# One sorted expert group with weights fetched per tile, in a two-layer decoder planned by hand

## The chip, the cores and the metric

The kernel runs on one core of one Trainium2 chip. The metric is the device time of one execution in microseconds (us); the figure for a kernel is the median over several executions. A run can also be profiled: the profile's span goes from the first to the last instruction, and the profiled execution has a device time of its own, slightly longer than its span.

The engines are TensorE (PE, matrix products; its weight loads are shown apart as PEld), VectorE (DVE), ScalarE (ACT), GpSimd (POOL) and SyncE (SP, which only issues transfers). Each engine runs its own list of instructions strictly in order and waits on semaphores for the others.

## The reference, cut to what matters

The computation is a pre-norm decoder of two layers on x[16, 128, 256], all in fp32:

```
x = x + L0_attn(ln(x));   x = x + L0_xattn(ln(x), ctx);   x = x + L0_ffn(ln(x))
x = x + L1_attn(ln(x));   x = x + L1_xattn(ln(x), ctx);   x = x + L1_ffn(ln(x))
```

The change touches only the last term, a mixture of 8 experts of which each token uses 2, beside one shared expert:

```
shared = swiglu(x, ws_gate, ws_up, ws_down)                   # inner width 256
scores = sigmoid(x @ gate_weight.T)                           # (tokens, 8)
w, idx = top_k(scores, 2);  w = 2.5 * w / (w.sum(-1) + 1e-20)
y[e]   = (silu(x @ w_gate[e].T) * (x @ w_up[e].T)) @ w_down[e].T   # inner width 128
out    = sum over the two chosen e of w * y[e]  +  shared
```

## The kernel before, in words

**Lanes.** The 16 sequences of 128 tokens are cut into 8 lanes of two sequences (256 tokens each). A lane passes through `layer_0` (causal attention, attention to the context, a block-sparse FFN) and `layer_1` (self attention, windowed attention to the context, then the experts). Every stage is a Python generator.

**The planner.** The order of the instructions on every engine is fixed when the kernel is built. The class `Turns` (lines 81 to 262) holds all running generators as threads. A thread asks for an engine and for tiles from numbered pools (`yield PE, dict(bank=1)`); `run` picks the thread that could start first by a table of costs (`charge`, `dve`, `act`, `pool`, `indexed`), and breaks ties in favour of threads that are in an attention score step (`holds`, or a request for the score banks `s`), then by rank. So costs, tile limits (`LIMITS`) and the tie rule decide the order on PE, DVE, ACT, POOL and SP; on the chip each engine then keeps that order whatever the true durations are. `IN_FLIGHT` lanes (five) run at a time, started in the order of `TURN`.

**Two forms of the experts.** Dense (`expert_ffn`): all eight experts are computed for all tokens of a lane. Per lane that is 8 experts times 4 fp32 products for gate and up, a product `wb` that spreads the routing weight over the inner width, and 16 products down; the shared expert's products run in the same loops. Sorted (`routing`, then `sorted_experts`): for a group of lanes, `routing` scatters each token's normalised row to its two experts' areas of a DRAM table (`to_experts`, four indexed transfers per lane, POOL) and computes the shared expert as a dense part (`shared`). When the group's last lane is routed, `plan` (DVE) works out which rows belong to which tile of 128 rows, and the group's tiles are started. The number of tiles is fixed at 2·(tokens)/128 + 7, to hold any distribution over the experts. With GROUPS ((0,1,2),(3,4,5)) there are two groups of 12 + 7 = 19 tiles, and lanes 6 and 7 are dense.

**One sorted tile** (`expert_tile`, before): POOL gathers 128 rows (1 KB each) into `xg`; PE transposes them (2), ACT copies to `xgT`; PE reads the tile's expert number from SBUF into a register (`value`, line 158, a TENSOR_LOAD) and uses it as the column offset into the resident weights `gu` (two products); ACT and DVE form silu(gate)·up; PE transposes (`hT2`), ACT copies; PE multiplies with the resident `down` at the same register offset; ACT copies to `yo` and issues its transfer to `by_experts`. The resident weights (three tiles of 1 MB) are loaded by `late_weights` when the last lane has left layer 0, and a group may not start before they have landed (`ready`).

**Combining** (`combining`): after a group's last tile, each lane gathers its tokens' two results from `by_experts` (four indexed transfers on POOL), DVE adds them into x with their weight, and SP writes x out.

`blank` clears `to_experts` in eight transfers per group, so that unused rows are finite.

Of the kernel before, what the change touches and what calls it, by code (L numbers as in the profile page):

```python
# [10 lines left out]
I32 = mybir.dt.int32  # L11
# [7 lines left out]
P = 128  # L19
DC = D // P  # L20
G = 2
# [9 lines left out]
BPC = P // 64  # L31
NE, TOPE = 8, 2

GROUPS = ((0,1,2),(3,4,5))


OUT = -(2.0**100)
# [44 lines left out]
class Turns:  # L82
# [3 lines left out]

    HOP = 70.0
    HOP_FROM_PE = 200.0  # L90
    SWITCH = 91.0

    def __init__(self, nc, limits):
        self.nc = nc
# [60 lines left out]
        self.moves = max(self.moves, self.now.at) + n_bytes / 300.0  # L155
        self.now.at = self.moves + 2000.0

    def value(self, src, most):

        self.charge(PE, 300.0)  # L160
        return self.nc.values_load(
            src, engines=(mybir.EngineType.PE,), min_val=0, max_val=most,
            skip_runtime_bounds_check_because="a count of the experts but one, times their width",
        )

    def indexed(self, out, out_index, src, src_index):

        at = lambda i: None if i is None else bass.IndirectOffsetOnAxis(ap=i, axis=0)
        self.charge(POOL, 1100.0 if out_index is not None else 1600.0)
        self.moved(4 * int(np.prod((src if src_index is None else out).shape)))  # L170
        self.nc.gpsimd.indirect_dma_start(out, at(out_index), src, at(src_index))  # L171

    def fetch(self, out, src):
# [58 lines left out]
    def run(self, more):  # L232

        while True:
            more()
            best = None
            for i, th in enumerate(self.threads):
                if th.ask is None:
                    continue
                engine, takes = th.ask  # L240
                at = self.reach(th, engine)
                ok = True
                for tag, n in takes.items():
                    left = sorted(self.tiles[tag])
                    if not n:
                        continue
                    if len(left) < n:
                        ok = False
                        break
                    at = max(at, left[n - 1])  # L250
                key = (at, not (th.holds or "s" in takes), th.rank, i)
                if ok and (best is None or key < best[0]):
                    best = key, th, at
            if best is None:
                assert not self.threads, "no thread can go on"
                return
            _, th, at = best
            engine, takes = th.ask
            for tag, n in takes.items():
                self.tiles[tag].sort()  # L260
                del self.tiles[tag][:n]
            th.at, th.last = max(th.at, at), engine
            self.resume(th, None)


class Thread:
    def __init__(self, gen, rank, at, parent):
        self.gen, self.rank, self.at, self.parent = gen, rank, at, parent
        self.holds = parent is not None and parent.holds
        self.last, self.ask, self.waits, self.children, self.result = None, None, 0, [], None  # L270


# [1 line left out]
def decoder(ctx: ExitStack, tc: tile.TileContext, a: dict, out: bass.AP):  # L274
# [83 lines left out]
    class Sorted:  # L358
# [3 lines left out]
        def __init__(self, k, lanes):  # L362
            self.lanes, self.left = lanes, len(lanes)
            self.cap = cap = len(lanes) * GT
            self.tiles = n = TOPE * cap // P + NE - 1
            self.to_experts = dram.tile([NE * cap + P, D], F32, name=f"to_experts{k}")
            self.by_experts = dram.tile([n * P, D], F32, name=f"by_experts{k}")

            self.first_row = keep.tile([P, NE], F32, name=f"first_row{k}")
            self.next_row = keep.tile([P, NE], F32, name=f"next_row{k}")  # L370
            self.offset = keep.tile([P, NE], F32, name=f"offset{k}")

            self.tile_rows = keep.tile([P, n], I32, name=f"tile_rows{k}")
            self.tile_expert = keep.tile([P, n], I32, name=f"tile_expert{k}")
# [7 lines left out]


    LIMITS = dict(
        bank=4, s=2, oT=1, xn=5, xT=4, qk=5, qs=3, kb=3, v=3, p=4, oS=2, on=4, xe=6, hm=7, tmp=3, rank=2, selT=2, p0=3,
        pT0=3, unseen=4, chosen=3, swap=1, words=1, top=3,
    )
    q = Turns(nc, LIMITS)

# [146 lines left out]
    def attention(qT, kb, v, j, unseen=None, to=None):  # L536
# [5 lines left out]

        js = slice(j * S, (j + 1) * S)
        yield PE, dict(s=2)
        q.now.holds = True
        ss = banks()
        for e in range(DC):
            for r in range(4):
# [9 lines left out]
        for t2, s in enumerate(ss):  # L558
# [5 lines left out]
        q.now.holds = False  # L564
        yield PE, dict(bank=1)
        t = bank([P, S], "topT")
        q.transpose(t, top, ident)
# [12 lines left out]
        )  # L580
        q.give("tmp")
        yield PE, dict(s=2)
        q.now.holds = True
        ss = banks()
        for e in range(DC):
            for h in range(HR):
# [10 lines left out]
        def exponentials(s):  # L597
            yield ACT, dict(p=1)
            p = new("p", [P, HC, S], "p")
            q.act("activation", p, s.rearrange("p r h e s -> p (r h e) s"), AF.Exp)  # L600
            q.give("s")
            q.now.holds = False
            return p

        pTs = yield [exponentials(s) for s in ss]
        q.now.holds = False
        yield PE, dict(oT=1, bank=1)

        oT = bank([P, H // 4, S], "oT")
# [14 lines left out]
        q.act("copy", oS, oT)  # L624
        q.give("oT")
        q.give("bank")
        q.now.holds = False
        yield PE, dict(bank=1)
        o = bank([P, H // 4, S], "o")
        for t4 in range(H // 4):  # L630
# [412 lines left out]
    def plan(g):  # L1043
# [35 lines left out]
        q.dve("tensor_scalar", f, f, consts[:, C_ROW : C_ROW + 1], None, ALU.add)  # L1079
        q.dve("tensor_copy", g.tile_rows, f)  # L1080
        q.dve("tensor_scalar", e, e, float(D), None, ALU.mult)
        q.dve("tensor_copy", g.tile_expert, e)
        q.give("tmp", 3)

    def expert_tile(g, i):

        yield POOL, dict(xe=2)
        xg = new("xe", [P, D], "xg")
        q.indexed(xg, None, g.to_experts, g.tile_rows[:, i : i + 1])
        yield PE, dict(bank=1)  # L1090
        t = bank([P, DC, S], "xgt")
        for d in range(DC):
            q.transpose(t[:, d, :], xg[:, d * P : (d + 1) * P], ident)
        q.give("xe")
        yield ACT
        xgT = new("xe", [P, DC, S], "xgT")
        q.act("copy", xgT, t)
        q.give("bank")
        yield PE, dict(bank=1, tmp=1)
        gu = bank([P, 2, P], "gu2")  # L1100
        at = q.value(g.tile_expert[0:1, i : i + 1], (NE - 1) * D)
        for d in range(DC):
            q.matmul(gu, xgT[:, d, :], w["gu"][d][:, bass.ds(at, D)], start=d == 0, stop=d == DC - 1)
        q.give("xe")
        yield ACT
        sg = new("tmp", [P, P], "sg2")
# [12 lines left out]
        hT = new("pT0", [P, P], "hT")  # L1119
        q.act("copy", hT, t)  # L1120
        q.give("bank")
        yield PE, dict(bank=1, xe=1)
        y = bank([P, D], "y2")
        q.matmul(y, hT, w["down"][:, bass.ds(at, D)], start=True, stop=True)
        q.give("pT0")
        yield ACT
        yo = new("xe", [P, D], "yo")
# [3 lines left out]
        q.give("xe")  # L1131

    def combining(g, l):

        yield DVE
        t = small.tile([P, G, TOPE, NE], F32, tag="picked", name="picked", bufs=2)
        each = g.offset.unsqueeze(1).unsqueeze(1).to_broadcast([P, G, TOPE, NE])
        q.dve("tensor_tensor", t, pick[l], each, ALU.mult)
        f = small.tile([P, G, TOPE], F32, tag="wk", name="from", bufs=2)
        q.dve("tensor_reduce", f, t, AX.X, ALU.add)  # L1140
        q.dve("tensor_tensor", f, f, place[l], ALU.add)
        by = results[l]
        q.dve("tensor_copy", by, f.rearrange("p j k -> p (j k)"))

        def one(j, k):
            yield POOL, dict(xe=1)
            y = new("xe", [P, D], "yg")
            q.indexed(y, None, g.by_experts, by[:, j * TOPE + k : j * TOPE + k + 1])
            yield DVE
            q.dve(  # L1150
                "scalar_tensor_tensor", x[l][:, j, :], y, weight[l][:, j, k : k + 1], x[l][:, j, :], ALU.mult, ALU.add
            )
            q.give("xe")

        yield [one(j, k) for j in range(G) for k in range(TOPE)]
        nc.sync.dma_start(out[l * G : (l + 1) * G].rearrange("b s d -> s b d"), x[l])

    def blank(g):
# [235 lines left out]
    def layer_1(l):  # L1394
# [4 lines left out]
        if g is not None:  # L1399
            yield from routing(l)  # L1400
            g.left -= 1
            if g.left == 0:
                q.start(sorted_experts(g), 2 * NL + min(g.lanes), max([q.now.at] + ready))

    IN_FLIGHT = 5

    TURN = [(0, l) for l in range(6)]
    for l in range(NL):
        TURN += [(1, l), (0, l + 6)] if l + 6 < NL else [(1, l)]

    def more():
        n = begun[0]
# [51 lines left out]
def _layout(i):  # L1464
# [10 lines left out]
    def both_ways(mask):  # L1475
# [54 lines left out]
```

## Time and profile before

| what | value |
|---|---|
| median of 8 runs | 839.28 us (837.53 to 841.04) |
| device time of the profiled execution | 839.29 us |
| span of the profiled execution | 837.5 us |
| PE busy, share of the span | 777.4 us, 93% |
| PE weight loads busy | 609.6 us, 73% |
| DVE / ACT / POOL busy | 478.2 us, 57% / 393.6 us, 47% / 434.7 us, 52% |
| mean granted PE clock | 0.975 |
| bytes moved by DMA | 65.98 MB, 79 GB/s on average |

How to read the page: a group of instructions is named by its source line, engine, operation and tiles (`gu<-gu,xgT` writes gu from gu and xgT; buffer numbers are left out). Most operations go through the planner's helpers, so many groups share one line: L132 is every matmul, L137 every transpose, L141 every DVE, L145 every ACT, L151 every POOL compute operation, L171 every indexed transfer, L161 the register load. An fp32 matmul is recorded as two passes, so counts of fp32 products are twice those of the code; transposes are one pass each. A record's mean duration includes the pipeline's latency: the pitch at which passes follow each other is read from the chain of waits or the timeline instead. "Idle before" is the time the engine stood still just before the group and what released it.

### The profile page before, as it was taken

The page shows a single profiled execution, that of the slowest core. Times are in us where ns is not written, and L with a number is a line of the kernel's source. Part 1 is how long each engine was busy: PE and PEld are TensorE (multiplying, and loading weights), DVE is VectorE, ACT ScalarE, POOL GpSimd, SP SyncE. Part 2 cuts the span into 40 slices and gives each one's busy share as a digit, 9 for nine tenths or more (in the row PEclk, how much of TensorE's full clock was granted, in tenths as well). Part 3 has the DMA queues.
Part 4 walks back from the last instruction along what each step waited for, and adds up shares of the span by engine and source line. Part 5 has one row for each costly group of instructions (what it writes and reads, how often), then busy time and mean ns, then how long its engine had stood idle before and what let it go on. Part 6 is the DMA issues. An engine that isn't in the chain of part 4 may idle for free.

```text
span 837.5 us, 19964 instructions
## 1 busy us (share of the span) xinstructions
PE 777.4 (93%) x7864; PEld 609.6 (73%) x7864; DVE 478.2 (57%) x1261; ACT 393.6 (47%) x899; POOL 434.7 (52%) x693
## 2 busy tenths in 40 slices
PE   6999999999999999999798998999999788999992
PEld 5777678788778777787576777777777575687782
DVE  4445746545437337655476546697677367374343
ACT  4545563443265546525643545455545643542430
POOL 5334665235135448556549429586687455472304
PEclk9999999999999999999899998999999997999997
DMA  8446522412700010120002131111132122242214
GB/s 288 143 129 173 155 68 84 150 51 73 238 4 1 14 52 3 40 81 9 1 14 77 52 114 52 52 45 58 40 92 68 45 83 76 64 132 70 89 47 124
DMA packets 63582, 65.98 MB, mean 79 GB/s; under 512 B 9024, under 2 KB 56256, under 8 KB 62848
## 3 DMA queue, kind: packets, MB, share of 16 engines
q1 hardware_dynamic: 53888, 48.43, 18.5%
q0 software_dynamic: 4128, 11.28, 4.4%
q10 hardware_dynamic: 5472, 4.98, 1.8%
q8 instruction: 63, 1.03, 0.5%
q14 instruction: 31, 0.25, 0.1%
HBM read 35.31 MB, written 25.17 MB: 72 GB/s over the span
## 4 chain that ended last, share of the span: by engine, by line
PE 70%; DVE 11%; POOL 8%; ACT 5%; issue 4%; DMA 2%; ACTq 0%; POOLq 0%; DVEq 0%
PE s L132 14%; PE y L132 9%; PE pj L132 9%; PE pr L132 8%; PE gu L132 8%; PE hp L132 7%; PE oT L132 4%; PE tps L137 2%; DVE top L141 2%; POOL rstd L151 2%; PE o L137 2%; PE rt L132 2%; ACT p L145 1%; DMA yg<-by_experts,results 1%; POOL qs L151 1%
## 5 line engine op out<-in xcount | busy, mean ns | idle before, releaser
L141 DVE TENSOR_REDUCE top<-s 128x8 f32<-128x1024 f32 x96 | 112.9, 1217 | 54.8 <-PE s L132 54.5
L145 ACT ACTIVATE p<-s 128x1024 f32<-128x1024 f32 x96 | 93.1, 1022 | 58.8 <-PE s L132 58.8
L151 POOL TENSOR_TENSOR qs<-qT,less 128x512 f32<-128x512 f32 x48 | 61.1, 1278 | 89.5 <-ACT less L145 89.3
L151 POOL TENSOR_SCALAR rstd<-mv 128x2 f32<-128x2 f32 x72 | 17.9, 248 | 103.3 <-DVE mv L141 92.7
L132 PE MATMUL hp<-srcT,L_w 128*128 128x256 f32 x256 | 67.2, 392 | 0.1
L132 PE MATMUL s<-kb,qT 32*128 32x256 f32 x768 | 60.0, 412 | 1.3 <-DVE top L141 0.7
L132 PEld LDWEIGHTS s<-qs,kb 32*128 32x128 f32 x1536 | 48.5, 186 | 16.4 <-issue 8.1
L132 PE MATMUL s<-qs,kb 32*128 32x128 f32 x1536 | 58.1, 283 | 2.4 <-POOL qs L151 1.4
L171 POOL DMA_INDIRECT xg<-to_experts,tile_rows x38 | 37.6, 991 | 40.8 <-PE xgt L137 17.9
L132 PE MATMUL y<-L_w,hm 128*128 128x256 f32 x256 | 58.8, 382 | 0.0
L141 DVE SCALAR_TENSOR_TENSOR sg<-sg,gu 128x128 f32<-128x128 f32 (+1 forms) x70 | 24.0, 343 | 57.5 <-ACT sg L145 57.4
L132 PE MATMUL oT<-p,v 128*32 128x128 f32 x1536 | 52.9, 279 | 2.8 <-ACT less L145 1.0
L151 POOL TENSOR_SCALAR kb<-kT,consts 128x256 f32<-128x256 f32 x96 | 53.1, 565 | 3.4 <-ACT kT L145 2.5
L151 POOL TENSOR_TENSOR rstd<-rstd,power 128x2 f32<-128x2 f32 x72 | 51.4, 714 | 6.0
L132 PEld LDWEIGHTS hp<-srcT,L_w 128*128 128x128 f32 x256 | 45.5, 194 | 11.4 <-issue 2.2
L132 PEld LDWEIGHTS y<-L_w,hm 128*128 128x128 f32 x256 | 47.7, 190 | 7.5 <-issue 1.5
L145 ACT ACTIVATE hm<-hp,cols 128x256 f32<-128x256 f32 x64 | 26.8, 470 | 54.6 <-PE hp L132 54.2
L145 ACT ACTIVATE sg<-gu 128x128 f32<-128x128 f32 (+1 forms) x70 | 22.8, 326 | 59.4 <-PE gu L132 54.6
L132 PEld LDWEIGHTS oT<-p,v 128*32 128x32 f32 x1536 | 39.5, 111 | 14.5 <-issue 5.7
L132 PEld LDWEIGHTS s<-kb,qT 32*128 32x128 f32 x768 | 37.5, 189 | 16.5 <-issue 7.8
L145 ACT COPY oS<-oT 128x512 f32<-128x512 f32 x48 | 28.2, 588 | 43.1 <-PE oT L132 43.1
L137 PE MATMUL tps<-consts,xn 128*128 128x128 f32 x224 | 36.2, 284 | 11.4 <-DVE xn L141 7.0
(209 smaller groups left out, 1801.1 us busy)
## 6 DMA issues: line engine op xcount, KB each, us to landing
to_experts<-zero SPq DMA_DIRECT2D x14, 768.0 KB, 4.2
unseen<-hidden SPq DMA_DIRECT2D x128, 64.0 KB, 2.1
by_experts<-yo ACTq DMA_DIRECT2D x38, 128.0 KB, 1.7
c<-in_ctx SPq DMA_DIRECT2D x16, 256.0 KB, 3.6
x<-in_x SPq DMA_DIRECT2D x8, 256.0 KB, 6.3
L_w<-in_L_w SPq DMA_DIRECT2D x2, 1024.0 KB, 6.8
hidden<-plain SPq DMA_DIRECT2D x32, 64.0 KB, 1.6
swap<-kT SPq DMA_DIRECT2D x16, 128.0 KB, 2.1
```

Of the source, the lines that this page charges most:

```text
L132: self.nc.tensor.matmul(out, lhsT, rhs, **kw)
L137: self.nc.tensor.transpose(out, src, ident)
L141: getattr(self.nc.vector, name)(out, *args, **kw)
L145: getattr(self.nc.scalar, name)(out, *args, **kw)
L151: getattr(self.nc.gpsimd, name)(out, *args, **kw)
L171: self.nc.gpsimd.indirect_dma_start(out, at(out_index), src, at(src_index))
```

## The change

1. **Groups.** One sorted group of lanes 0 to 4 (2·1280/128 = 20, plus 7: 27 tiles) instead of two of three lanes (38 tiles); lanes 5, 6 and 7 are dense.
2. **Weights by indexed transfer.** A new input `L1_experts` holds each expert's gate, up and down weights as 128 rows of 3 KB. `plan` computes row numbers (`tile_weights` = 128·expert + partition) instead of a column offset (`tile_expert`). Each sorted tile gathers 128 x 3 KB of weights on POOL into a `p` buffer of 4 KB per partition, then gathers its tokens into the last 1 KB of the same buffer; the result `yo` overwrites the tokens, and the buffer is given back after the result's transfer. The register load on PE (`value`) is gone. The resident weights stay for the dense lanes.
3. **Combining** uses one `p` buffer per lane instead of four `xe` tiles.
4. **Planner.** Threads no longer carry `holds`; a request for `s` counts as 200 ns earlier (`LEAD`); PE is charged 40 ns more per turn (`PART`); an indexed transfer costs 1050 ns on POOL, and 2 us more until it is counted as landed. LIMITS: qs 3 to 2, p 4 to 6, xe 6 to 3, hm 7 to 5, tmp 3 to 4.
5. **Start order.** TURN starts seven lanes of layer 0 before the first of layer 1 (six before); the sorted group no longer waits for the resident weights.

```diff
-GROUPS = ((0,1,2),(3,4,5))
+GROUPS = ((0, 1, 2, 3, 4),)
...
+    LEAD = 200.0
+    PART = 40.0
...
-    def value(self, src, most):
-        self.charge(PE, 300.0)
-        return self.nc.values_load(...)
...
     def indexed(self, out, out_index, src, src_index):
-        self.charge(POOL, 1100.0 if out_index is not None else 1600.0)
+        self.charge(POOL, 1050.0)
         self.moved(4 * int(np.prod((src if src_index is None else out).shape)))
+        self.now.at += 2000.0
...
-                key = (at, not (th.holds or "s" in takes), th.rank, i)
+                first = "s" in takes
+                key = (max(at - self.LEAD * first, self.free_at[engine] - first), not first, th.rank, i)
...
+            if engine == PE:
+                self.free_at[PE] += self.PART
...
-        bank=4, s=2, oT=1, xn=5, xT=4, qk=5, qs=3, kb=3, v=3, p=4, oS=2, on=4, xe=6, hm=7, tmp=3, rank=2, selT=2, p0=3,
-        pT0=3, unseen=4, chosen=3, swap=1, words=1, top=3,
+        bank=4, s=2, oT=1, xn=5, xT=4, qk=5, qs=2, kb=3, v=3, p=6, oS=2, on=4, xe=3, hm=5, tmp=4,
+        rank=2, selT=2, p0=3, pT0=3, unseen=4, chosen=3, swap=1, words=1, top=3,
...
     def expert_tile(g, i):
-        yield POOL, dict(xe=2)
-        xg = new("xe", [P, D], "xg")
+        yield POOL, dict(p=1)
+        we = new("p", [P, HC, S], "we").rearrange("p h s -> p (h s)")
+        xg = yo = we[:, 3 * D :]
+        q.indexed(we[:, 0 : 3 * D], None, a["L1_experts"], g.tile_weights[:, i : i + 1])
+        yield POOL
         q.indexed(xg, None, g.to_experts, g.tile_rows[:, i : i + 1])
...
-        at = q.value(g.tile_expert[0:1, i : i + 1], (NE - 1) * D)
         for d in range(DC):
-            q.matmul(gu, xgT[:, d, :], w["gu"][d][:, bass.ds(at, D)], start=d == 0, stop=d == DC - 1)
+            wt = we[:, d * D : (d + 1) * D].rearrange("p (n f) -> p n f", f=P)
+            q.matmul(gu, xgT[:, d, :], wt, start=d == 0, stop=d == DC - 1)
...
-        q.matmul(y, hT, w["down"][:, bass.ds(at, D)], start=True, stop=True)
+        q.matmul(y, hT, we[:, DC * D : 3 * D], start=True, stop=True)
...
     def combining(g, l):
+        yield POOL, dict(p=1)
+        y = new("p", [P, G * TOPE, D], "yg")
         def one(j, k):
-            yield POOL, dict(xe=1)
-            y = new("xe", [P, D], "yg")
-            q.indexed(y, None, g.by_experts, by[:, j * TOPE + k : j * TOPE + k + 1])
+            yield POOL
+            q.indexed(y[:, i, :], None, g.by_experts, by[:, i : i + 1])
...
-                q.start(sorted_experts(g), 2 * NL + min(g.lanes), max([q.now.at] + ready))
+                q.start(sorted_experts(g), 2 * NL + min(g.lanes), q.now.at)
...
-    TURN = [(0, l) for l in range(6)]
+    TURN = [(0, l) for l in range(7)]
     for l in range(NL):
-        TURN += [(1, l), (0, l + 6)] if l + 6 < NL else [(1, l)]
+        TURN += [(1, l), (0, l + 7)] if l + 7 < NL else [(1, l)]
...
+    by_expert = lambda w: w.transpose(2, 0, 1, 3).reshape(NE, P, DC * D)
+        "L1_experts": np.concatenate([by_expert(gate_up), down.transpose(0, 2, 1)], 2).reshape(NE * P, 3 * D),
```

More of the change, by code (lines that the diff above doesn't have):

```diff
@@ L156, in moved @@
         self.now.at = self.moves + 2000.0
-    def value(self, src, most):
-        self.charge(PE, 300.0)
[L161 to L164, printed above, removed]
     def indexed(self, out, out_index, src, src_index):
         at = lambda i: None if i is None else bass.IndirectOffsetOnAxis(ap=i, axis=0)
-        self.charge(POOL, 1100.0 if out_index is not None else 1600.0)
+        self.charge(POOL, 1050.0)
         self.moved(4 * int(np.prod((src if src_index is None else out).shape)))
+        self.now.at += 2000.0
         self.nc.gpsimd.indirect_dma_start(out, at(out_index), src, at(src_index))
@@ L268, in __init__ @@
         self.gen, self.rank, self.at, self.parent = gen, rank, at, parent
-        self.holds = parent is not None and parent.holds
         self.last, self.ask, self.waits, self.children, self.result = None, None, 0, [], None
@@ L373, in __init__ @@
             self.tile_rows = keep.tile([P, n], I32, name=f"tile_rows{k}")
-            self.tile_expert = keep.tile([P, n], I32, name=f"tile_expert{k}")
+            self.tile_weights = keep.tile([P, n], I32, name=f"tile_weights{k}")
     groups = [Sorted(k, lanes) for k, lanes in enumerate(GROUPS)]
@@ L544, in attention @@
         yield PE, dict(s=2)
-        q.now.holds = True
         ss = banks()
@@ L563, in attention @@
             q.give("s")
-        q.now.holds = False
         yield PE, dict(bank=1)
@@ L582, in attention @@
         yield PE, dict(s=2)
-        q.now.holds = True
         ss = banks()
@@ L601, in exponentials @@
             q.give("s")
-            q.now.holds = False
             return p
         pTs = yield [exponentials(s) for s in ss]
-        q.now.holds = False
         yield PE, dict(oT=1, bank=1)
@@ L626, in attention @@
         q.give("bank")
-        q.now.holds = False
         yield PE, dict(bank=1)
@@ L1078, in plan @@
         q.dve("scalar_tensor_tensor", f, e, float(g.cap), f, ALU.mult, ALU.add)
[L1079 to L1082, printed above, removed]
+        for to, v in ((g.tile_rows, f), (g.tile_weights, e)):
+            if v is e:
+                q.dve("tensor_scalar", v, v, float(P), None, ALU.mult)
+            q.dve("tensor_scalar", v, v, consts[:, C_ROW : C_ROW + 1], None, ALU.add)
+            q.dve("tensor_copy", to, v)
         q.give("tmp", 3)
     def expert_tile(g, i):
-        yield POOL, dict(xe=2)
-        xg = new("xe", [P, D], "xg")
+        yield POOL, dict(p=1)
[3 more added lines that the diff above has]
+        yield POOL
         q.indexed(xg, None, g.to_experts, g.tile_rows[:, i : i + 1])
@@ L1093, in expert_tile @@
             q.transpose(t[:, d, :], xg[:, d * P : (d + 1) * P], ident)
-        q.give("xe")
-        yield ACT
+        yield ACT, dict(xe=1)
         xgT = new("xe", [P, DC, S], "xgT")
@@ L1121, in expert_tile @@
         q.give("bank")
-        yield PE, dict(bank=1, xe=1)
+        yield PE, dict(bank=1)
         y = bank([P, D], "y2")
-        q.matmul(y, hT, w["down"][:, bass.ds(at, D)], start=True, stop=True)
+        q.matmul(y, hT, we[:, DC * D : 3 * D], start=True, stop=True)
         q.give("pT0")
         yield ACT
-        yo = new("xe", [P, D], "yo")
         q.act("copy", yo, y)
@@ L1130, in expert_tile @@
         q.load(g.by_experts[i * P : (i + 1) * P, :], yo, engine=ACT)
-        q.give("xe")
+        q.give("p")
     def combining(g, l):
@@ L1143, in combining @@
         q.dve("tensor_copy", by, f.rearrange("p j k -> p (j k)"))
+        yield POOL, dict(p=1)
+        y = new("p", [P, G * TOPE, D], "yg")
         def one(j, k):
-            yield POOL, dict(xe=1)
-            y = new("xe", [P, D], "yg")
-            q.indexed(y, None, g.by_experts, by[:, j * TOPE + k : j * TOPE + k + 1])
+            i = j * TOPE + k
+            yield POOL
+            q.indexed(y[:, i, :], None, g.by_experts, by[:, i : i + 1])
             yield DVE
             q.dve(
-                "scalar_tensor_tensor", x[l][:, j, :], y, weight[l][:, j, k : k + 1], x[l][:, j, :], ALU.mult, ALU.add
+                "scalar_tensor_tensor", x[l][:, j, :], y[:, i, :], weight[l][:, j, k : k + 1], x[l][:, j, :], ALU.mult, ALU.add
             )
-            q.give("xe")
         yield [one(j, k) for j in range(G) for k in range(TOPE)]
+        q.give("p")
         nc.sync.dma_start(out[l * G : (l + 1) * G].rearrange("b s d -> s b d"), x[l])
```

## The prediction

> **What bounds the kernel now.** I read the page first, then busy time by stage, then the groups of the expert part, the chain of waits near the end, and POOL's waits.
>
> ```profile
> PE 777.4 (93%) x7864; PEld 609.6 (73%) x7864; DVE 478.2 (57%) x1261; ACT 393.6 (47%) x899; POOL 434.7 (52%) x693
> ```
>
> PE is the bound. The stages (start:end, length, busy time of PE, PEld, DVE, ACT, POOL, granted clock, DMA share, GB/s) show where it isn't:
>
> ```profile
> 0.00:40.00 40.00, 31.41 (x156) 26.27 (x157) 19.95 (x75) 18.48 (x47) 17.36 (x51) 1.00 0.64 213
> 40.00:400.00 360.00, 354.21 (x3925) 280.14 (x3924) 197.71 (x474) 172.83 (x374) 173.76 (x286) 1.00 0.26 78
> 400.00:420.00 20.00, 15.84 (x180) 11.46 (x179) 7.59 (x16) 11.17 (x22) 10.01 (x20) 0.83 0.01 2
> 420.00:560.00 140.00, 132.27 (x1449) 103.24 (x1448) 91.59 (x230) 71.55 (x147) 87.18 (x139) 0.96 0.18 59
> 560.00:640.00 80.00, 76.13 (x964) 57.21 (x962) 58.26 (x150) 42.25 (x94) 57.15 (x81) 1.00 0.21 66
> 640.00:740.00 100.00, 88.03 (x814) 65.69 (x813) 57.26 (x181) 50.98 (x135) 54.44 (x78) 0.93 0.21 67
> 740.00:822.00 82.00, 79.07 (x386) 65.57 (x385) 41.69 (x129) 26.31 (x83) 29.00 (x34) 1.00 0.28 86
> 822.00:837.50 15.50, 0.43 (x3) 0.03 (x1) 4.12 (x9) 0.00 (x0) 5.80 (x6) 0.62 0.42 128
> ```
>
> Idle PE: 8.6 us at the start, 5.8 until 400, 27.8 from 400 to 740 (4.2 + 7.7 + 3.9 + 12.0), 2.9 until 822, and 15 at the end. In the stages from 400 to 740 the clock was also partly halved: (1 - clock) x length / 0.5 gives 6.8 + 11.2 + 14 = 32 us at half clock, which cost up to 16 us. Some 44 us thus hang on the order of the instructions.
>
> The expert groups (busy us, mean ns of one | idle before, its releasers):
>
> ```profile
> L132 PE MATMUL gu<-gu,xgT 128*128 x152 | 41.2, 400 | 2.0 <-ACT xgT L145 1.4 <-ACT yo L145 0.4
> L132 PE MATMUL gu<-srcT,gu 128*128 128x256 f32 x128 | 30.8, 385 | 1.4 <-DVE hm L141 0.5 <-ACT yo L145 0.4 <-ACT hT L145 0.2
> L132 PE MATMUL y<-down,hT 128*128 x76 | 23.9, 406 | 1.6 <-ACT gained L145 0.7 <-ACT hT L145 0.6 <-DVE x L141 0.3
> ```
>
> Chain of waits near the end (start, us, what):
>
> ```profile
> 805.43 1.99 PE gu L132 x8
> 807.42 0.43 PE y L132 x2
> 807.85 0.11 PE hT L137
> 807.96 1.73 PE gu L132 x8
> ...
> 823.53 3.98 DMA yg<-by_experts,results
> ...
> 828.66 3.31 DMA yg<-by_experts,results
> 832.07 0.48 DVE x L141
> ```
>
> Passes follow each other every 0.216 us (1.73/8), transposes every 0.11. After PE's last work at 822.4 the end hangs on the second group's gathers of results.
>
> **The change part by part.** I sum against the profiled execution: 839.3 us, its span of 837.5 plus 1.8 outside; the median is the same 839.3.
>
> *Fewer tiles.* Per tile PE runs 2 + 1 transposes and 4 + 2 passes (counts 152/38 and 76/38): 3 x 0.11 + 6 x 0.216 = 1.63 us. Eleven tiles fewer: -17.9.
>
> *One lane more dense.* Per dense lane 64 passes gu (128/2), 32 passes down and 8 `wb` of 0.11: 96 x 0.216 + 0.9 = 21.6 us; the shared expert is computed either way. +21.6. PE's work thus grows by 3.7.
>
> *No register load.* 38 loads, each 302 ns in PE's load queue.
>
> ```profile
> L161 PEldq TENSOR_LOAD <-tile_expert x38: 295/302/576, 569.7 to 801.5; - x38
> ```
>
> They are issued ahead and run beside the products: before the first pass on a tile's weights the timeline shows anything from no gap (740.07, 0.216 after the pass before) to about 0.3 (735.61). Bounds: 0 and 38 x 0.302 = 11.5. I take 0.1 a tile, nearer to the rows with no gap: -4. The Trainium skill ("DMA: Bandwidth & Descriptors", Latency and other measured facts) gives such a load a floor of about 600 ns; by it, bare, this term would be an estimated -23 and the total 811. The row is half of that, and is mostly hidden.
>
> *The tail.* In the new order the group's last product `y2` stands in front of 160 fp32 passes and eight `wb`: 160 x 0.216 + 0.9 = 35.4 us of PE work (lane 6's down products and the whole of lane 7). Last on DVE is lane 7's sum, not a gathered result. In the trace the dense lane's last sum ended at 823.3, the last gathered one at 832.55, and both are followed only by the transfer of x: -9.2. What hides the gathers: copy, issue and landing of the last `yo` 0.4 + 0.3 + 1.7, then 20 gathers at a pitch of 1.25 us (they started at 814.78, 816.02, 817.28), landing 2.9 us after issue, last sum 0.5: 2.4 + 19 x 1.25 + 2.9 + 0.5 = 29.6 us, under 35.4 by 5.8. If the last tile is later than that, each us counts. DVE has 20 x 0.48 + some 12 us of the lane's own work in this time, in one queue: a sum that waits for its gather holds up the `hm` behind it, which the down products need. 0 to +3, I take +1.
>
> *Weights by transfer.* 27 x 393 KB = 10.6 MB. Queue q0 moved 11.28 MB in 4.4% of 16 engines' span, that is 37 us of all of them; so some 35 us more, spread over the 120 us of the tiles, where the DMA share is 0.21 to 0.28: it rises to about 0.55. The order puts five weight gathers in front of four of their tokens' gathers, and up to six buffers are in use; the landing (between 2.8 us, `xg` of 128 KB, and 6.8, a plain load of 1 MB; I take 4, a third of the way up in size) is hidden under other tiles and dense passes. Price 0; bare it would be 4 us a tile, 108 in all, and the first tile alone is 4.
>
> *POOL's queue.* 94 indexed transfers (54 + 20 + 20) for 86 (38 + 24 + 24): +8 x 1.25 = 10 us on an engine that is 52% busy. Each weight gather may wait at POOL's head for a `p` buffer, and behind it stand the tokens' gathers, `rstd` of normalisations, `eq`/`gt` of the routing and `qs` and `kb` of the last attentions. Before, the same form of wait stood there (from 560 to 800: total, times, longest):
>
> ```profile
> POOL xg L171 <- PE xgt L137: 17.9, 5, 8.5
> ```
>
> It held POOL, while PE's idle time in that stretch was mostly put to ACT and DVE. I take 0 for the difference; -5 to +20.
>
> *SP.* Half as many clearing transfers (8 for 16, 10.6 MB for 12.6) between 37 and 222 us, where PE is 98% busy: 0. The three weight loads stay.
>
> *The order.* Everything moves on every engine. I compared, in the two built orders, how much PE work (at the row's pitch) lies between a step of an attention and the PE step that needs its result through another engine: maxima (2 x 1.22 on DVE plus hops: 2.6 us needed), `qs` (2 x 0.37 + 1.28: 2.2), exponentials (2 x 1.02: 2.2), `oS` (0.59: 0.75). Too short before: 2, 3, 7, 1 places, lacking 7.6 us in sum; after: 0, 9, 6, 4, lacking 7.3. So no gain and no loss is visible. Eleven tiles fewer save some of PE's waits for `xgT`, `h` and `hT` (1.4 + 1.3 + 0.6, times 11/38): -1. Bounds: half of the 44 us either way, -22 to +22.
>
> Sum: 839.3 - 17.9 + 21.6 - 4 - 9.2 + 1 + 0 - 1 = 829.8, say **830**.
>
> **The rivals.** *R1, POOL's queue becomes the bound of the tile stretch (slower).* Weight gathers wait for `p` buffers that attention's exponentials (two at a time) and unfinished tiles hold. For it: the wait above; POOL's 57 of 80 us from 560 to 640; 54 gathers instead of 38. Against it: after the last attention only normalisations and routing of three lanes share the queue. Price: the 17.9 us grow with 54/38 and with the second wait per tile to about 35; it decides once PE runs out of dense passes behind a waiting tile, which I put at 25 us exposed, and two more stretches at half clock like the one after PE's 6.2 us wait near 410 (6.8 us, half lost): 830 + 25 + 7 = 862 at the hard end, 845 to 850 with half of it. The skill ("TensorE: Matmul & The Clock Gate", Part 1) says an idle window of about 3.4 us halves the clock; this trace shows 0.83 in 400 to 420 beside that wait, so it agrees.
>
> *R2, the order gives the tail back.* The tail goes, but the stretch from 400 to 740, now without layer 0's FFN as filler until the tiles begin, idles 8 to 11 us more: 838 to 841. For it: DVE and POOL are busy 65% and 62% from 420 to 560 already. Against: covers are alike.
>
> *R3, the order gains as well.* The three stalls before 740 (4.2, 7.7 and 12.0 us idle, with the half clock) shrink to the 1.6% idle of 40 to 400: -15: 815.
>
> *R4, the change doesn't do what it says:* the register load costs nothing and the fixed 27 tiles need as much waiting as 38; the tail alone remains: 830 + 4 + 1 = 835, still faster.
>
> **How the numbers follow.** Forecast (822 to 837, R4 included) 0.50; R3 0.14; R2 0.10; R1 0.26. Without a term for the order, the forecast's own range is 822 to 837; with R3's and half of R1's end, the range is 813 to 852. The measurement can tell 0.2%, 1.7 us: faster means under 837.6. Forecast and R3 lie there, and little of R2: 0.65; within 0.2% most of R2: 0.07; slower 0.28.
>
> **What would show it.** The tail: last PE work within 6 us of the span's end, and no `yg` gather in the chain's last steps. Work: `gu<-we,xgT` x108, `gu<-srcT,gu` x192. Register load: no gap before a tile's first pass. Weights: no long PE wait whose releaser is `we`. POOL: long waits of `we` gathers with PE idle in the same windows would be R1; a stretch from 400 to 560 with more than 12 us idle would be R2. I am wrong if the tile stretch idles more than 25 us, or if the gathers of results still end the kernel.

## The result, and the profile after

The changed kernel takes **841.24 us** (median of 19 runs, 839.06 to 842.56); the kernel before took 838.60 in the 56 runs beside it. The ratio is **1.0028, interval 1.0018 to 1.0038**: slower by 0.3%, a little more than the 0.2% that a measurement of this kernel can tell. The forecast was 830 and faster. The time lies in the range of 813 to 852, the sign is wrong.

The profiled execution has a span of 840.0 us (before 837.5). The page of after, engines and the queue of the indexed transfers (packets, MB, share of 16 engines' span):

```profile
PE 783.4 (93%) x7866; PEld 615.3 (73%) x7866; DVE 469.7 (56%) x1232; ACT 386.9 (46%) x864; POOL 446.3 (53%) x700
...
q0 software_dynamic: 5376, 19.40, 7.4%
```

PE has two instructions more than before and 6 us more busy time, POOL 11.6 us more. The stages of after, same columns as before:

```profile
0.00:40.00 40.00, 32.46 (x158) 27.17 (x159) 21.67 (x81) 19.02 (x50) 15.42 (x47) 1.00 0.63 206
40.00:400.00 360.00, 349.78 (x3756) 274.61 (x3755) 180.76 (x417) 166.56 (x357) 162.19 (x265) 0.99 0.23 70
400.00:420.00 20.00, 18.73 (x129) 15.90 (x131) 13.89 (x51) 5.39 (x12) 8.95 (x17) 1.00 0.35 126
420.00:560.00 140.00, 132.72 (x1693) 102.35 (x1692) 95.76 (x235) 81.71 (x167) 107.30 (x170) 1.00 0.15 48
560.00:640.00 80.00, 72.43 (x941) 55.27 (x941) 58.11 (x161) 43.98 (x86) 49.06 (x76) 1.00 0.14 46
640.00:740.00 100.00, 88.43 (x779) 67.43 (x779) 46.88 (x119) 43.51 (x115) 62.44 (x79) 0.93 0.41 131
740.00:822.00 82.00, 75.46 (x365) 61.83 (x364) 45.29 (x153) 25.53 (x79) 38.22 (x48) 0.98 0.38 118
822.00:840.00 18.00, 13.42 (x62) 10.71 (x60) 7.37 (x19) 1.15 (x3) 2.75 (x3) 1.00 0.23 73
```

PE now works to the end (13.4 of the last 18 us, before 0.4 of 15.5). The stall at 400 to 420 is gone. But 640 to 740 is no better than before (88.4 us busy, clock 0.93), and POOL is busy there for 62 us instead of 54. The last steps of the chain of waits:

```profile
823.16 3.22 DMA yg<-by_experts,results
...
826.41 0.48 DVE x L143
826.89 0.35 DVE hm L143
...
827.28 8.91 PE y L134 x40
```

The gathers of results end under PE's work, and forty passes of the dense lanes are the last thing on PE. From the last PE work (836.2) to the end it is 3.8 us; before it was 15.1. So the tail is gone as forecast. Some 10 of its 11 us were lost elsewhere, and PE's own work grew by 3.8.

To see where, I charged every PE instruction with the pitch of its kind (the 30th percentile of the distance to the next) and took the sum from each stage's length. What is left is PE's lost time: idle, half clock, late starts. Kernels of the experiments below stand beside it, all from their profiled executions. Read the table across: the level of a row hangs on the pitch charged for the attention's packed products (another reading of it puts 140 to 400 of before at 23.7 instead of 11.0), while differences between columns move by less than 2 us.

| stage, us | before | after | e12b: no weight gathers | e15: no gathers for tiles | e13: a second gather each |
|---|---|---|---|---|---|
| 0 to 40 | 12.9 | 12.4 | 12.2 | 12.2 | 11.4 |
| 40 to 140 | 4.2 | 14.3 | 13.4 | 13.4 | 13.6 |
| 140 to 400 | 11.0 | 12.9 | 12.9 | 13.0 | 12.7 |
| 400 to 560 | 25.2 | 15.0 | 16.1 | 16.1 | 15.6 |
| 560 to 640 | 9.0 | 13.3 | 13.2 | 13.0 | 14.2 |
| **640 to 690** | 11.0 | **18.1** | 11.4 | 12.9 | **27.2** |
| 690 to 740 | 14.1 | 4.4 | 4.3 | 4.2 | 5.2 |
| **740 to 800** | 5.6 | **10.3** | 5.7 | 7.4 | **14.8** |
| 800 to the last PE instruction | 1.0 | 3.2 | 3.0 | 3.1 | 4.3 |
| after it | 15.4 | 4.2 | 4.2 | 4.1 | 4.3 |
| POOL busy, 640 to 690 | 28.5 | 35.4 | 29.0 | 19.7 | 39.8 |

PE's work itself grew from 728.0 to 731.8, +3.8. In after, the chain of waits runs through POOL where the first tiles start (start us, us, what):

```profile
655.31 2.18 POOL kb L153 x4
...
657.65 0.22 POOL we L166
657.88 1.18 issue
659.05 0.61 POOL we L166
659.66 1.08 issue
660.74 0.95 POOL we L166
...
669.13 1.01 POOL we L166
670.16 0.42 POOL eq L153
...
671.03 1.27 POOL qs L153
672.35 2.19 PE s L134 x48
```

Between an attention's `kb` and its `qs` POOL issues tile transfers one behind the other, and PE's score products wait for `qs` at the end of that line. This gave theory **Q1**: the 27 weight gathers cost by POOL's issue time, 1.25 us each in front of `rstd`, `qs`, `kb` and `eq`. The rivals: **Q2**, their 10.6 MB and their landing; **O**, the new order of everything, which has nothing to do with the gathers.

### The profile page after: what moved, and what is told of

It is laid out like the page before. It is cut to its first block, busy times and chain, and to the rows that moved or that the text cites. A ratio compares the mean times of both kernels' runs of the same rounds, so it can differ in the third digit from the quotient of the medians.

```text
span 840.0 us, 19669 instructions
## 1 busy us (share of the span) xinstructions
PE 783.4 (93%) x7866; PEld 615.3 (73%) x7866; DVE 469.7 (56%) x1232; ACT 386.9 (46%) x864; POOL 446.3 (53%) x700
## 4 chain that ended last, share of the span: by engine, by line
PE 67%; POOL 11%; DVE 10%; ACT 5%; issue 5%; DMA 2%; POOLq 0%; ACTq 0%; DVEq 0%
PE s L134 14%; PE pj L134 10%; PE y L134 9%; PE pr L134 9%; PE gu L134 7%; PE hp L134 7%; PE oT L134 4%; PE tps L139 2%; POOL rstd L153 2%; ACT p L147 2%; PE o L139 2%; POOL we L166 1%; DVE top L143 1%; PE rt L134 1%; DVE st L143 1%
## 5 line engine op out<-in xcount | busy, mean ns | idle before, releaser
L147 ACT ACTIVATE p<-s 128x1024 f32<-128x1024 f32 x96 | 95.4, 1026 | 48.6 <-PE s L134 44.5
L134 PE MATMUL s<-qs,kb 32*128 32x128 f32 x1536 | 60.0, 285 | 8.2 <-POOL qs L153 4.5
L134 PE MATMUL s<-kb,qT 32*128 32x256 f32 x768 | 61.9, 414 | 2.3 <-ACT p L147 2.2
L147 ACT ACTIVATE sg<-gu 128x256 f32<-128x256 f32 (+1 forms) x67 | 22.8, 341 | 77.1 <-PE gu L134 72.9
L147 ACT ACTIVATE less<-topT,consts 128x128 f32<-128x128 f32 x96 | 29.6, 371 | 47.8 <-PE topT L139 47.6
L134 PE MATMUL gu<-srcT,gu 128*128 128x256 f32 x192 | 47.5, 394 | 2.7 <-DVE hm L143 1.2
L134 PEld LDWEIGHTS oT<-p,v 128*32 128x32 f32 x1536 | 40.1, 112 | 12.2 <-issue 8.1
L166 POOL DMA_INDIRECT we<-in_L_experts,tile_weights x27 | 26.6, 984 | 41.5 <-ACT sg L147 11.4
L139 PE MATMUL tps<-consts,xn 128*128 128x128 f32 x224 | 36.0, 282 | 11.9 <-DVE xn L143 10.3
```

Of the source, the lines that this page charges most:

```text
L134: self.nc.tensor.matmul(out, lhsT, rhs, **kw)
L139: self.nc.tensor.transpose(out, src, ident)
L147: getattr(self.nc.scalar, name)(out, *args, **kw)
```

## The experiments

**Take the weight gathers away.** e1 keeps the changed kernel's order and charges the planner the same, but issues no weight gather:

```diff
-        q.indexed(we[:, 0 : 3 * D], None, a["L1_experts"], g.tile_weights[:, i : i + 1])
+        q.charge(POOL, 1050.0)
+        q.moved(4 * P * 3 * D)
+        q.now.at += 2000.0
...
+            q.matmul(gu, xgT[:, d, :], w["gu"][d][:, i % NE * D : (i % NE + 1) * D], ...)
```

> The changed kernel in its own order, with the 27 weight gathers left out on POOL; the tiles multiply with resident weights at fixed columns (expert i mod 8), so the output is not the reference's. Theory Q (POOL's queue): the chain through POOL between 651 and 672 us of the changed kernel (weight gathers in front of rstd, kT, kb and qs) loses ten gathers of 1.25 us, and the routing's eq no longer stands behind two gathers near 757 and 766: 8 to 14 us faster than the changed kernel's 841.2, so 827 to 833. Rival O (the order everywhere, from the new rule of the planner and the start order): within 2 us of 841.

Measured 831.73 beside 838.14 for before, ratio 0.9933 (0.9908 to 0.9958). That is 9.5 us under the changed kernel's 841.24, which ran beside a before of 838.60. Until 640 the two traces agree; the gain is in 640 to 690 and 740 to 800, the two bold rows.

**Is the register load free?** e3 is the kernel before with fixed columns in place of the register:

```diff
-        at = q.value(g.tile_expert[0:1, i : i + 1], (NE - 1) * D)
+        q.charge(PE, 300.0)
+        at = i % NE * D
...
-            q.matmul(gu, xgT[:, d, :], w["gu"][d][:, bass.ds(at, D)], start=d == 0, stop=d == DC - 1)
+            q.matmul(gu, xgT[:, d, :], w["gu"][d][:, at : at + D], start=d == 0, stop=d == DC - 1)
...
```

> The kernel before in its own order, with the 38 register loads and the register offsets left out; the tiles use fixed columns (expert i mod 8), so the output is not the reference's. My term for the load: -4 us (834.6). If the load is hidden everywhere: 838.6. If each is bare: -11.5, 827.

838.66 beside 838.14, ratio 1.0002 (0.9991 to 1.0013): the 38 loads cost nothing that can be measured, 1 us at most by the interval.

**The version without either cost.** e12 has the changed kernel's order and single group, but reads the resident weights at a register's offset, as before.

```diff
-        q.indexed(we[:, 0 : 3 * D], None, a["L1_experts"], g.tile_weights[:, i : i + 1])
+        q.charge(POOL, 1050.0)
+        q.moved(4 * P * 3 * D)
+        q.now.at += 2000.0
...
+        at = nc.values_load(g.tile_expert[0:1, i : i + 1], engines=(mybir.EngineType.PE,), ...)
+            q.matmul(gu, xgT[:, d, :], w["gu"][d][:, bass.ds(at, D)], ...)
```

> The changed kernel's order, one sorted group of five lanes and 27 tiles, but the expert's weights taken from the resident copy at an offset in a register again, and no weight gathers. Computes what the reference does. Theory Q1 with a register load that is hidden (1.0002 in e3): 830 to 834, faster than both kernels. Rival: in the new order, with more passes in a row in front of the load, 27 loads of 0.302 us show: up to 840.

This run, with e8, e9 and e10, fell on a chip on which every kernel is slower: before took 853.43 us there, e12 852.56 (0.9991, 0.9974 to 1.0007). Its trace agrees with e1's until 640, loses some 6 us more from 640 to 800, and thereafter has 18.6 us of waits in its chain that the profile can't name. The chain of e12:

```profile
803.91 6.72 another core or an unknown queue
...
812.86 11.85 another core or an unknown queue
```

So ratios from that chip say little of single terms, and I ran the kernels that mattered again beside the changed kernel:

> The changed kernel itself, beside the others of this call on the same chip, because on the chip of e8, e9, e10 and e12 the kernel before took 853 us for 838, and no run of the changed kernel stands beside them there. Both theories: a ratio to before of 1.002 to 1.004.

> The kernel of e12 again (the changed kernel's order, weights from the resident copy by a register's offset, no weight gathers; computes what the reference does), beside the changed kernel on the same chip. Theory Q1 (27 weight gathers on POOL's queue cost some 9 us, a register load nothing): 0.988 to 0.992 of the changed kernel's time, about 832 on a chip where before takes 838. Rival (register loads show in the new order): 0.993 to 1.000 of it.

a2: 841.68, ratio 1.0026 (1.0012 to 1.0039), as in the first measurement. e12b: **832.01, ratio 0.9922 (0.9902 to 0.9942)**, that is 0.9885 of the changed kernel (832.01/841.68). It is the version that beats both, by 6.6 and 9.7 us. Register loads are free in the new order too.

**Issue time or bytes?** e8 keeps the 27 issues and cuts the bytes to a twelfth (its products read resident weights, as in e1); e9 keeps the bytes and takes the issue off POOL. Both charge the planner as e1 does.

```diff
(e8)
-        q.indexed(we[:, 0 : 3 * D], None, a["L1_experts"], g.tile_weights[:, i : i + 1])
...
+        nc.gpsimd.indirect_dma_start(we[:, 0:64], None, a["L1_small"], bass.IndirectOffsetOnAxis(ap=g.tile_weights[:, i : i + 1], axis=0))
(e9)
-        q.indexed(we[:, 0 : 3 * D], None, a["L1_experts"], g.tile_weights[:, i : i + 1])
...
+        nc.sync.dma_start(we[:, 0 : 3 * D], a["L1_experts"][i % NE * P : (i % NE + 1) * P, :])
```

> The changed kernel with its 27 weight gathers cut to 64 floats a row (32 KB for 393 KB), the order of issue unchanged; the expert products read resident weights of a fixed expert, so the output is not the reference's. POOL's issue time and its place in the queue stay, the bytes go. Theory Q1 (the 9.5 us that e1 took away were POOL's time at the head of its queue, 27 x 1.25 us in front of rstd, qs, kb and eq): 838 to 842, as the changed kernel. Rival Q2 (they were the 10.6 MB on the DMA engines and the landing of we): 830 to 834, as e1. In between, 835 to 837, means both.

> The changed kernel with its 27 weight transfers of 393 KB issued as plain transfers on SP's queue (of a fixed expert, tile number modulo 8, so the output is not the reference's), the order otherwise unchanged, the products on these buffers as in the changed kernel. The bytes, the buffers and the landing stay; POOL's issue time goes. Theory Q1: 829 to 835, as e1. Rival Q2: 838 to 843, as the changed kernel. SP's queue takes a wait for a buffer at its head, in front of loads that come later in the kernel; if that decides, over 843.

On the slow chip: e8 858.75 (1.0051, 1.0025 to 1.0078), e9 853.37 (1.0000, 0.9978 to 1.0022), e12 852.56. The ranges in us are missed by all, as they were written for the ordinary chip; the distances (e8 6.2 us over e12, e9 0.8) spoke for Q1. Then on an ordinary chip, with a third kernel that doubles the issues:

```diff
(e13, behind each weight gather)
+        more = small.tile([P, 64], F32, tag="more", name="more", bufs=8)
+        nc.gpsimd.indirect_dma_start(more, None, a["L1_small"], bass.IndirectOffsetOnAxis(ap=g.tile_weights[:, i : i + 1], axis=0))
```

> The kernel of e8 again (the changed kernel's 27 weight gathers cut to 32 KB each, order unchanged, products on resident weights of a fixed expert; not the reference's output), now beside the changed kernel on the same chip. Theory Q1 (POOL's issue time): 0.997 to 1.003 of the changed kernel's time. Rival Q2 (bytes and landing): 0.986 to 0.992 of it.

> The kernel of e9 again (the 393 KB a tile moved by plain transfers from SP's queue, of a fixed expert; not the reference's output), beside the changed kernel on the same chip. Theory Q1: 0.987 to 0.993 of the changed kernel's time. Rival Q2: 0.997 to 1.003.

> The changed kernel with a second indexed transfer of 64 floats a row (32 KB, into a buffer that nothing reads) behind each of its 27 weight gathers: POOL's issue time for them doubled, 10.6 MB grown by 0.9. Theory Q1: as much again as the first ones cost, 1.008 to 1.016 of the changed kernel's time (848 to 855 where it takes 841). Rival Q2: 0.998 to 1.003.

> The changed kernel itself, for the ratios of the other three on the same chip: 1.002 to 1.004 of before on a chip where before takes 838; on a chip like that of the first run of e8, where before takes 853, theory Q1 expects 1.006 to 1.010, by e8's 1.005 and e12's 0.999 there.

| kernel | us | ratio to before (interval) | ratio to a3 |
|---|---|---|---|
| a3, the changed kernel | 842.50 | 1.0034 (1.0020 to 1.0048) | 1 |
| e8b, issues without bytes | 841.29 | 1.0026 (1.0008 to 1.0044) | 0.9986 |
| e9b, bytes without POOL's issues | 833.75 | 0.9930 (0.9906 to 0.9954) | 0.9896 |
| e13, issues doubled | 856.69 | 1.0200 (1.0168 to 1.0232) | 1.0168 |

All as Q1 has it, e13 slightly beyond it (14.2 us, for the 7 to 14 expected). The bytes are worth 1.2 us (e8b against a3), which the intervals can't tell from nothing. The stage from 640 to 690 of after, e12b, e8b, e9b and e13, one fence each (columns as in the stages above):

```profile
640.00:690.00 50.00, 41.31 (x331) 30.05 (x331) 22.77 (x56) 20.86 (x55) 35.42 (x46) 0.86 0.41 133
```

```profile
640.00:690.00 50.00, 43.75 (x364) 33.05 (x364) 25.59 (x63) 22.66 (x61) 28.98 (x37) 0.97 0.26 78
```

```profile
640.00:690.00 50.00, 41.42 (x333) 30.74 (x334) 22.40 (x55) 20.56 (x56) 35.63 (x47) 0.86 0.24 73
```

```profile
640.00:690.00 50.00, 42.32 (x355) 31.42 (x355) 22.61 (x61) 21.64 (x59) 29.85 (x39) 0.97 0.48 148
```

```profile
640.00:690.00 50.00, 33.39 (x217) 23.82 (x217) 18.39 (x47) 16.54 (x45) 39.83 (x51) 0.80 0.40 118
```

PE's clock is low where POOL is busy for 35 us or more (0.86, 0.86 and 0.80), and it doesn't go by the bytes: e9b moves most (148 GB/s) and has 0.97, e8b moves 73 GB/s and has 0.86. Under 30 us of POOL it doesn't go by POOL either: 0.97 in e12b, and 0.93 in e15 with 19.7. Who waits for POOL's small operations, from 635 to 800 (us in total, times, longest), in e12b, after and e13:

```profile
DVE xn L143 <- POOL rstd L153: 4.8, 6, 1.2
...
ACT xn L147 <- POOL less L153: 4.2, 3, 3.2
...
DVE rank L143 <- POOL gt L153: 0.8, 1, 0.8
```

```profile
DVE xn L143 <- POOL rstd L153: 8.6, 7, 2.4
...
ACT xn L147 <- POOL less L153: 8.2, 4, 4.4
...
DVE rank L143 <- POOL gt L153: 4.2, 3, 2.3
```

```profile
DVE xn L143 <- POOL rstd L153: 20.2, 7, 7.8
ACT xn L147 <- POOL less L153: 16.8, 4, 7.2
...
DVE rank L143 <- POOL gt L153: 9.7, 3, 4.4
```

Sums of 9.8, 21.0 and 46.7 us with 27, 54 and 81 tile transfers: the waits grow faster than the transfers. They are on DVE and ACT, and PE's own list of waits shows only their ends (`tps` for `xn`, `s` for `qs`).

A rival within POOL is the wait for a free `p` buffer at the head of its queue. The traces speak against it: from 635 to 800 POOL stood still in front of its `we` gathers, other than for issue, 32.4 us in e12b, 39.8 in after and 24.1 in e13. The slowest kernel has the least, and e13's second gathers take no `p` buffer.

**Did the gathers that the change took away cost as much?** If so, the netting of the prediction (94 for 86) was sound. e14 moves the 38 token gathers of the kernel before to plain transfers on SP, e15 the 27 that are left in e12b; the planner is charged as it was:

```diff
-        q.indexed(xg, None, g.to_experts, g.tile_rows[:, i : i + 1])
...
+        nc.sync.dma_start(xg, g.to_experts[i % NE * g.cap : i % NE * g.cap + P, :])
```

> The kernel before with its 38 gathers of tokens moved off POOL: each is a plain transfer of 128 fixed rows on SP's queue (not the reference's output); order, buffers and bytes unchanged. Theory N (an indexed transfer on POOL costs about the same wherever it stands in this stretch; by the stretch from 640 to 800, 11.4 us for 26 of them, 0.44 us each): 38 x 0.44 = 17 us less at most, 822 to 832, so that the 27 new ones of the change were largely paid for by the 15 that it took away. Theory F (only the new kernel's crowd from 635 to 690 costs, before's queue has room): 836 to 839. SP's queue gets a wait for a buffer in front of loads of attention: if that decides, over 840.

> The kernel of e12b with its 27 gathers of tokens moved off POOL in the same way (fixed rows by plain transfers on SP's queue; not the reference's output). No indexed transfer is left on POOL for the tiles. Theory N: 27 x 0.44 = 12 us less than e12b's 832, 818 to 824. Theory F: the first 27 taken away had freed the queue, 829 to 833.

e14: 836.83 beside 838.49, ratio 0.9984 (0.9968 to 0.9999); e15: 831.81, ratio 0.9913 (0.9892 to 0.9934), against e12b's 0.9922. Theory F: 38 gathers of the old order cost 1.7 us (0.1 to 2.7 by the interval), the 27 token gathers of the new order nothing measurable, and 27 more on top 9.7. (SP's queue has new waits in both; e14 lost 1.8 us less than before from 640 to 690, and 2.2 more from 560 to 640, and what of the latter is SP's was not separated.) In the last row of the table, POOL at 20 to 29 us of 50 costs PE the same (11 to 13 us lost in the stage); at 35 it costs 18, at 40 it costs 27.

**The order by itself.** Five kernels change only what the planner decides by, or the grouping:

> The kernel before, with only the planner's new rule (LEAD 200 for requests of the score banks, no holds, 40 ns per PE turn); groups, tiles, limits, start order and POOL costs stay. Rival O: the rule alone costs what the change lost, 5 to 10 us: 844 to 849. Theory Q: the rule is about neutral, 834 to 842.

> The kernel before with one sorted group of five lanes and three dense lanes; resident weights, register loads, planner, limits and start order as before. By my terms: +3.7 PE work, -1 for eleven register loads, -9 to -11 for the tail: 830 to 833 (theory Q: the loss came with the weight gathers). Rival O': the grouping itself costs what the tail gives, because tiles come too late to fill the attention of lanes 3 to 5: 838 to 842.

> The changed kernel with the planner's old rule for the choice among threads (a thread that holds its rank first, no lead of 0.2 us for the attention's products, no 0.04 us added to each PE piece); everything else as changed. If the new rule is worth something by itself in the changed kernel, this is slower than the changed kernel by 3 us or more. If the rule is a shuffle (theory O: any change of the order moves the stalls by plus or minus 20), it may fall to either side: 825 to 865. If it does nothing, within 2 us of the changed kernel.

> The changed kernel; the planner charges POOL what the trace shows (1.25 us for an indexed transfer, 1.35 with the scatter, for 1.05; 0.08 us more for each other POOL instruction), so that it sees POOL's queue fill in 578 to 680. Theory Q1 with a planner that can mend it: 833 to 839. Theory O: the new order's stalls decide, 825 to 865, and nothing is learned of POOL unless the stretch from 640 to 690 shows it: PE work there over 43 us for 41.3.

> The changed kernel with one line of the planner changed: a gather (it takes a p buffer and POOL) is chosen as if it came 2.5 us later, so that rstd, qs, kb and eq which are due within that time go in front of it on POOL. Theory Q1 (what costs is that these stand behind gathers): 832 to 838. Rival O (each change of the planner's order moves the stalls elsewhere, as the order alone did in e2, +19, and the grouping alone in e5, +34): outside of 828 to 842, to either side.

```diff
(e2, on before; e4 is the reverse on after, with `holds` back)
+    LEAD = 200.0
+    PART = 40.0
...
-                key = (at, not (th.holds or "s" in takes), th.rank, i)
+                first = "s" in takes
+                key = (max(at - self.LEAD * first, self.free_at[engine] - first), not first, th.rank, i)
...
+            if engine == PE:
+                self.free_at[PE] += self.PART
(e5, on before)
-GROUPS = ((0,1,2),(3,4,5))
+GROUPS = ((0, 1, 2, 3, 4),)
(e7, on after)
-        ns = 200 + (2.15 if two else 1.42) * self.width(out, args)
+        ns = 280 + (2.15 if two else 1.42) * self.width(out, args)
...
-        self.charge(POOL, 1050.0)
+        self.charge(POOL, 1350.0 if out_index is not None else 1250.0)
(e10, on after)
+                back = 2500.0 * (engine == POOL and "p" in takes)
-                key = (max(at - self.LEAD * first, self.free_at[engine] - first), not first, th.rank, i)
+                key = (max(at - self.LEAD * first, self.free_at[engine] - first) + back, not first, th.rank, i)
```

| kernel | us (before beside it) | ratio to before (interval) |
|---|---|---|
| e2, before with the new rule | 857.13 (838.14) | 1.0222 (1.0198 to 1.0247) |
| e5, before with one group of five | 872.28 (838.14) | 1.0415 (1.0392 to 1.0437) |
| e4, after with the old rule | 873.72 (838.59) | 1.0417 (1.0394 to 1.0440) |
| e7, after with POOL's measured costs | 866.45 (838.59) | 1.0323 (1.0299 to 1.0347) |
| e10, after with gathers standing back | 863.02 (853.43) | 1.0110 (1.0077 to 1.0143) |

e2, e5, e4 and e7 are 19, 34, 32 and 25 us slower than the kernel that they start from; e10 ran on the slow chip, where it stands 4.3 us above e8, which has the same issues. The loss isn't only where the edit aims. e5 loses most of it before 640, while its first tile's gather is issued at 671. Two of its stretches (before in the first: PE 58.8 us busy at clock 1.00; in the second: 34.9 at 0.91):

```profile
300.00:360.00 60.00, 47.66 (x573) 35.95 (x571) 26.24 (x76) 26.04 (x55) 32.92 (x54) 0.89 0.08 24
...
400.00:440.00 40.00, 30.83 (x401) 20.95 (x399) 20.42 (x35) 14.72 (x30) 21.27 (x27) 0.81 0.05 16
```

e10 had the group's results gathered last: its last PE instruction starts at 835.5, and the span is 861.3. e7 was to let the planner see POOL's queue, but the stage from 640 to 690 lost 25 us for 18. So e7 and e10 say nothing of Q1, and theory O is right in this: each of the five small edits to what the order is made by made its kernel slower, by 4 to 34 us. It does not explain the 9.7 us between two kernels of one order.

## Why the prediction was wrong, step by step

- **POOL's queue, 0: the step that failed.** It counted eight transfers more on an engine busy half of the time and took no cost. The netting was wrong (e14): all 38 tile gathers of the kernel before cost 1.7 us where they stood, so eleven fewer save next to nothing (the four result gathers and four scatters fewer were not tried), and the 27 new ones cost 9.7 us. The change puts all 54 tile transfers between 635.8 and 777.2: 54 x 1.25 = 67 us of these 141, in front of the `rstd`, `qs` and `kb` of the last attentions. Before, 38 were spread over 235 us (559.4 to 794.8), a share of 20% for 48%. That average hides stretches of 36% (12 gathers from 687 to 729) and 41% (14 from 752 to 795); by the second, the last attention's `qs` (719) and the last `rstd` (741) were done. This suggests that the number to look at was POOL's demand in the stretch, together with what still stands behind it, and not its count over the kernel. This is rival R1 in its place and its sign, at a third of its price: 6.7 us in 640 to 690 and 4.6 in 740 to 800 (after against e12b, profiled executions), for the 25 plus 7 put there. R1 expected the waits for `p` buffers to cost; e13 and the waits beside it show that POOL's own issue time does. R1 also misread a line: PE's wait of 6.2 us is the one at the kernel's start, and near 410 it waited 3.5 us.
- **No register load, -4:** measured 0 (e3, e12b). The rows with no gap were the right ones.
- **The tail, -9.2:** from the last PE instruction's start to the end 15.4 us became 4.2, -11.2. Right, 2 us too small.
- **Combining on DVE, +1:** 2.2 us more lost between 800 and PE's last instruction. Right, also in the mechanism: from 800 to 837 DVE's sums waited 6.3 us for gathers, and PE 1.9 us for the `hm` behind them. For this reason `yg` still stands in the chain's last steps, where the prediction expected none.
- **Fewer tiles and one dense lane, +3.7:** PE's work grew by 3.8. The counts are as said:

```profile
L134 PE MATMUL gu<-srcT,gu 128*128 128x256 f32 x192 | 47.5, 394 | 2.7 <-DVE hm L143 1.2
```

- **Weights by transfer, 0:** right for the bytes (e8b). The gathers' issue and landing in after:

```profile
L166 POOL DMA_INDIRECT we<-in_L_experts,tile_weights x27: 941/949/1387, 635.8 to 776.0; - x27
...
DMA to landing us min/median/max: 3.6/3.9/4.8
```

  The 4 us put for the landing were right; the DMA share rose to 0.41, not to 0.55.
- **SP, 0:** not tried. The stretch from 40 to 140, where the clearing transfers lie, lost 10 us more than before, but the waits that the trace lists for PE there are for ACT and DVE, none for a transfer.
- **The order, -1:** near in the sum, and by luck. Without the weight gathers (e12b), the rows of the table up to 800 differ from before by -0.7, +9.2, +1.9, -9.1, +4.2, +0.4, -9.8 and +0.1, which is -3.8. The gains from 400 to 560 and from 690 to 740 are R3's, the loss at 40 to 140 was in no rival and its cause stays open. Cover counts could not have told this, and the single edits (+4 to +34) show how wide the bounds had to be.

With the register at 0 and the tail at -11.2, the forecast's own sum is 829.8 + 4 - 2 = 831.8, and e12b took 832.0. With 9.7 for POOL it is 841.5, and the changed kernel took 841.2. With the order at -3.8, combining at 2.2 and the work at 3.8 as well it is 830.3, beside 830.0 of e12b's profiled execution; the closer agreement of the first sum is chance. R2 came nearest in its number (838 to 841), but by a mechanism that the trace contradicts: 400 to 560 lost 15.0 us, less than before's 25.2. The test "wrong if the tile stretch idles more than 25 us" missed it: from 640 to 800 PE idled 8.7 + 2.9 + 5.3 = 17 us, but at a clock of 0.86 in the first 50 and 0.97 in the last 60, which is up to (1 - clock) x length = 7.0 + 1.8 us more.

## What to carry to other kernels

An engine that issues transfers beside its own work is one queue for both: add up its demand in the stretch where the change puts it, with everything that stands behind it, and don't set it off against demand that the change removes elsewhere. Test for bytes and for issue apart, by moving the same bytes from another queue and by issuing the same number with few bytes. When the order is planned, keep it fixed in an experiment (charge the planner as before), or the reshuffle hides the effect.

## What the runs showed of the hardware

- An indexed transfer of 128 rows held POOL for 0.95 us, and 0.30 lay before the next, whether a row had 256 B (median 944 ns, e13), 1 KB (950) or 3 KB (949). The Trainium skill ("DMA: Bandwidth & Descriptors", Issuing engines are not separate DMA queues) says of starting transfers on several engines that it saves only the sequencer's time, "usually small relative to the DMA itself". Here it was 1.25 us of POOL beside a landing of 3.9, and yet nearly all of the cost: e9b, with the same bytes sent by SP, took 8.7 us less, because POOL had other work behind its issues.
- In after, short waits of PE were followed by half clock. From 650 to 656 PE was busy for 3.25 us, its longest single gap was 1.0 us, and from 656 to 666 the granted clock was 0.50 while PE was busy for 9.5 us. It was 0.50 again from 673 to 676, after a gap of 2.6 us. Half of these 12.5 busy us, some 6 us, went to the clock, beside 8.7 us of idle time in the stage.
- One chip ran every kernel 15 to 20 us slower than the others (before 853.4 for 838.6, e12 852.6 for 832.0), and e12's trace there has waits of 6.7 us on ACT and 11.9 us on DVE that no recorded event ended. What it is stays open. Times from it were compared only with times from it.
